# A four-layer hybrid block on one Trainium2 core: feed-forward weights unpacked in halves inside the last full phase, and a new order of the first two and last two phases

## The chip, the cores and the metric

The kernel runs on one core of one Trainium2 chip. Its time is the device time of one execution in microseconds (us). The engines named below are TensorE (PE, matmuls), VectorE (DVE), ScalarE (ACT), GpSimd (POOL) and the queue that issues the DMAs (SP). Each has its own stream of instructions and takes them in order; an instruction waits at the head of its stream until what it reads has been written and what it overwrites has been read.

## What is computed

The input x is 2 sequences of 512 tokens with 512 values each, in fp32. Four layers follow one another, each with a layer norm ahead and a residual sum behind:

```python
x = x + attn_a(layernorm(x))   # one 512x512 matmul with a block mask, and a bias
x = x + ffn(layernorm(x))      # silu(x@gate) * (x@up) @ down, weights stored as integers
x = x + attn_b(layernorm(x))   # the mixer: a state-space layer
x = x + ffn(layernorm(x))      # the same weights again
```

The feed-forward weights are unpacked as `(w - zero) * scale`, zero and scale per 128 rows; gate and up are 512x1792 each, down is 1792x512. In the mixer:

```python
gate, hBC, dt = split(x @ in_proj_w.T)     # 8192, 8192 + 2*8*128, 128 columns
hBC = silu(causal_conv4(hBC) + conv_b)
x, B, C = split(hBC)                       # 128 heads of 64; 8 groups of 128
dt = softplus(dt + dt_bias); A_dt = -exp(A_log) * dt
acs = cumsum(A_dt, within chunks of 128)
y = (tril(C B^T) * exp(acs_l - acs_s)) @ (x*dt)   # within a chunk
  + C @ state * exp(acs)                          # from the chunks before
  + D * x
y = y * rsqrt(mean(y^2) + eps) * norm_w * silu(gate)
return y @ out_proj_w.T
```

The factor rsqrt(mean(y^2) + eps) is one number per token, so the kernel applies it after the output projection, once the sum of squares over all 8192 values is known.

## The kernel before, in words

All four layers are one launch. `x_sb` holds the 1024 tokens in 8 tiles of 128 (t = 0 to 3 are sequence b = 0, 4 to 7 are b = 1), and `xn_t` the normalized input, transposed. `norm` (L102) makes statistics (L107, L109), the root on ACT (L111), the reciprocal (L114) and the scaled tile `tmp` (L121) on DVE; `turn` (L129) transposes it on PE into `ln_tr` (L134) and copies it to `xn_t` on ACT (L135). Most large projections go through `seven` (L169), the seven products of Strassen-Winograd in place of eight; its matmuls are all L177, its sums of products are L189 (ACT copy), L192, L197, L198, L206 and L211 (DVE).

The mixer (L532) works in phases. The 8192 inner channels are 64 tiles of 128; a phase takes two of them (j = 0, 1) for both sequences, so there are 32 phases. A phase's units are the four pairs (j, b). The loop over ph is software-pipelined: while the x columns of phase ph are projected and convolved (`x_front`; taps on DVE, L592, first tap on ACT, L589; silu L607), the tokens of phase ph - 1 are transposed (`x_tokens`, L685, L689, L693), its states formed (`states`, L706 to L717), its decay matrices (`half_scores`: `scores` with m on ACT, L747, L754, and DVE, L755, ce on ACT and POOL, L757, L761) and its scans done (`scan`: py, L774 and L783; y and gt, L793 and L794), and phase ph - 2 goes through the output projection (`out_project`, po, L808, added to `x_sb` by L818). The gates' stage of a phase (`g_front`: `seven` into `gt`, then silu) closes it. B and C belong to groups of eight channel tiles; a new group's `c_t`, `b_t` and `gm` are made every four phases (`group`, `group_scores`, L629 to L637). Squares of y are added up on POOL (`squares`, L800, L801).

The first phases stand ahead of the loop: `decays` (L557) makes the cumulative sums of a sequence and two exponentials of them, `step_sizes` the dt of the second sequence. The last phase (ph = 32, `front` false) breaks out of the loop and is written out below it: output projections of phase 30 (`outs`), scans of phase 31, `last_outs` (the output projections of phase 31), `factors` (L1064: ms, the sums of squares over 8192 on PE, L1067; root L99; reciprocal L100), `residual` (L1076: load of the stored input `x_d`, then L1079), and the norms of the next layer (`rest`, `ahead`). The second feed-forward layer then begins with pg and pu (L403) on slab 0 (256 columns), made from the weights that `first` holds. `dequant` (L222) loads integers, zeros and scales with three DMAs, subtracts on DVE (L230) and multiplies on POOL (L231).

The order on PE, ACT and DVE is the order in which the program names the instructions (`manual_schedule`, L1166). POOL's instructions and the DMAs on SP are ordered by the scheduler, from their priorities and from when their buffers come free. PSUM has three named sets of banks: `tr` (2), `proj` (3) and `yo` (3). `weights()` gives one of three 512 KB weight tiles, `room()` one of three 128x512 `tmp` tiles.

Of the kernel before, what the change touches and what calls it, by code (L numbers as in the profile page):

```python
# [8 lines left out]
F32 = mybir.dt.float32  # L9
# [28 lines left out]
def kernel(  # L38
# [210 lines left out]

    def now(q_compute):  # L250
        q, compute = q_compute
        compute()
        return q
# [229 lines left out]
    dt = keep.tile([P, NT, H], F32, tag="dt", name="dt")  # L483

    acs = keep.tile([P, NT, H], F32, tag="acs", name="acs")
# [46 lines left out]
    def mixer(waiting, step_args, loaded):  # L532

        with ExitStack() as st:
# [22 lines left out]
            def decays(b):  # L557

                cs = slice(b * NCH, (b + 1) * NCH)
                acs_t = room()  # L560
                pt = psum.tile([H, SEQ], F32, tag="tr", name="pacs")
                for c in range(NCH):
                    nc.tensor.matmul(
                        pt[:, c * P : (c + 1) * P],
                        lhsT=acs[:, b * NCH + c, :],
                        rhs=tri,
                        start=True,
                        stop=True,
                    )
                nc.scalar.copy(acs_t, pt)  # L570
                nc.sync.dma_start(acs_d[:, b * SEQ : (b + 1) * SEQ], acs_t)
                pa = psum.tile([P, NCH, H], F32, tag="yo", name="pa", bufs=3)
                pl = psum.tile([P, NCH, H], F32, tag="yo", name="pl", bufs=3)
                nc.tensor.matmul(pa, lhsT=tri, rhs=acs[:, cs, :], start=True, stop=True)
                nc.tensor.matmul(pl, lhsT=ones, rhs=acs[:, cs, :], start=True, stop=True)
                nc.scalar.copy(acs[:, cs, :], pa)
                nc.vector.tensor_tensor(
                    dec[:, b], pl[:, : NCH - 1], acs[:, b * NCH : (b + 1) * NCH - 1, :], ALU.subtract
                )
                nc.scalar.activation(e_last[:, b], pl[:, 1 : NCH - 1], AF.Exp)  # L580
                nc.scalar.activation(dec[:, b], dec[:, b], AF.Exp)
# [221 lines left out]
            def out_project(ph, ts, gts, wo):  # L803
                for t in ts:
                    b, c = divmod(t, NCH)
                    po = psum.tile([P, DIM], F32, tag="yo", name="po", bufs=3)
                    for j in range(PP):
                        nc.tensor.matmul(  # L808
                            po,
                            lhsT=gts[j, b][:, c * P : (c + 1) * P],  # L810
                            rhs=wo[:, j, :],
                            start=(j == 0),
                            stop=(j == PP - 1),
                        )
# [22 lines left out]
            decays(0)  # L837
# [3 lines left out]
            turn(waiting.pop(0))  # L841
            two_quarters(slice(SEQ - P, SEQ))
# [13 lines left out]
            decays(1)  # L856
# [3 lines left out]
            next(steps_bc)  # L860
            half_scores(0, 0, heads, ces)
# [4 lines left out]
            next(steps_bc)  # L866
            drain(3)
            next(steps_bc)
# [3 lines left out]
            half_scores(3, 0, heads, ces)  # L872
            run(steps_bc)
            gate, later = g_front(wg, gts)
            next(gate)
            drain(3)
# [3 lines left out]
            drain(3)  # L880
# [17 lines left out]
            first = []  # L898

            def scratch(shape):  # L900
                return [wrk.tile(shape, ty, tag="bc", name=nm, bufs=3) for nm, ty in (("wi", I32), ("zi", I32), ("sf", F32))]

            def scratch_up(shape):
                return [
                    pool.tile(shape, ty, tag=tag, name=nm)
                    for pool, tag, nm, ty in (
                        (sc, "wo", "wi", I32),
                        (keep, "dt", "zi", I32),
                        (keep, "acs", "sf", F32),
                    )  # L910
                ]

            for ph in range(1, n_ph + 1):
# [46 lines left out]
                wg = load_pair(c0, c0 + 1)  # L960
                if new_group:
                    wbc = load_group((c0 + PP) // CTG)
# [35 lines left out]
                finish(scans)  # L998
# [7 lines left out]
                for k in range(4):  # L1006
                    between(2 * k)
                    flush()
                    if last or k:
                        back_scores(4 + k)  # L1010
                    if last:
                        drain(1 if k < 3 else 0)
                    if made and k in (1, 2):
                        group_scores(made, groups[c0 // CTG], [k - 1])
                    between(2 * k + 1)
                    if last:
                        drain(1 if k < 3 else 0)
# [13 lines left out]
                if last:  # L1031
                    gate, later = g_front(wg, gts_new)
                finish(half_scan(units[2:], "proj" if new_group else "yo"))
                if last:
                    next(gate)
                half_scores(0, c0, heads_new)
                if last:
                    next(gate)
                drain(3)
# [47 lines left out]
            def last_outs(t):  # L1087
                out_project(n_ph - 1, [t], gts, wo_last)
# [3 lines left out]
            outs(0)  # L1092
            flush()
# [152 lines left out]
```

## Time and profile before

| what | value |
|---|---|
| time, three runs | 2327.41, 2327.43, 2330.75 us (median 2327.43) |
| the profiled execution's own time | 2327.67 us |
| its span in the profile | 2325.8 us (1.87 us lie around it) |
| mean granted PE clock | 0.996 |
| PE busy | 2296.2 us (99%) |
| DVE busy | 1607.5 us (69%) |
| ACT busy | 1155.2 us (50%) |
| POOL busy | 992.0 us (43%) |
| bytes moved by DMA | 201.41 MB |

The span runs from the first to the last recorded instruction. An engine's busy time is the part of the span in which it has an instruction in work. A line of the timeline gives start, duration, engine, line of the kernel, operation, output and inputs, the shape of both and how many instructions are taken together; brackets at its end hold the idle time just before it and what ended it. The mixer's first phase begins near 326 us, its last stage near 1998 us, and pg of the last feed-forward layer starts at 2050.14 us. The granted clock (PEclk) is TensorE's, 1.00 being full speed.

### The profile page before, as it was taken

What the parts mean: (1) busy time and instruction counts of PE and PEld (TensorE: products, weight loads), DVE (VectorE), ACT (ScalarE), POOL (GpSimd) and SP (SyncE); (2) the same over time, 40 slices, a digit from 0 to 9 for tenths busy, and PEclk for the clock granted to TensorE, in tenths of its full rate; (3) what the DMA queues carried; (4) which work ended last, traced back from release to release, by engine and by line L of the source; (5) the groups of instructions that cost most, each with busy time, mean ns of one, the idle gap of its engine ahead of it and who ended that gap; (6) DMA issues with size and microseconds to landing.
All of it is one profiled execution on the core that took longest, in us unless ns stands there. A gap on an engine that the chain in (4) does not pass through costs nothing.

```text
span 2325.8 us, 27474 instructions
## 1 busy us (share of the span) xinstructions
PE 2296.2 (99%) x9680; PEld 1214.3 (52%) x9680; DVE 1607.5 (69%) x2814; ACT 1155.2 (50%) x2460; POOL 992.0 (43%) x963
## 2 busy tenths in 40 slices
PE   9999998999999999999999999999999999899999
PEld 5444454555555555555555555555555555544444
DVE  5454148788788787877877887878778788755510
ACT  4111046656656665666565656556665666521100
POOL 2764013544544454444454444444453443346500
PEclk9999999999999999999999999999999999999999
DMA  5663012222222222222222222221222222346500
GB/s 185 191 200 100 23 55 77 73 73 73 73 82 64 73 82 73 64 73 82 68 69 81 73 65 78 78 73 64 82 72 65 75 71 73 91 141 216 176 14 23
DMA packets 145673, 201.41 MB, mean 87 GB/s; under 512 B 7040, under 2 KB 91904, under 8 KB 145536
## 3 DMA queue, kind: packets, MB, share of 16 engines
q1 hardware_dynamic: 145536, 199.66, 27.0%
q8 instruction: 77, 1.26, 0.2%
q14 instruction: 60, 0.49, 0.1%
HBM read 194.91 MB, written 4.72 MB: 86 GB/s over the span
## 4 chain that ended last, share of the span: by engine, by line
PE 95%; DVE 2%; DMA 1%; ACT 1%; issue 0%; SPq 0%; DVEq 0%; ACTq 0%
PE proj L177 39%; PE po L808 19%; PE yo L177 10%; PE ffn_o L453 8%; PE py L774 5%; PE pst L706 4%; PE py L783 3%; PE x_tr L685 2%; PE pg L403 1%; PE pu L403 1%; PE bs_o L305 1%; PE pgm L636 1%; DVE xc L592 1%; PE ln_tr L134 1%; DMA wi<-in_up_w_dram 0%
## 5 line engine op out<-in xcount | busy, mean ns | idle before, releaser
L761 POOL TENSOR_TENSOR ce<-ce,c_t 128x384 f32<-128x384 f32 x256 | 266.9, 1047 | 452.5 <-ACT ce L757 445.5
L808 PE MATMUL po<-wo,gt 128*128 128x512 f32 x992 | 436.8, 595 | 0.0
L177 PE MATMUL proj<-xn_t,w 128*128 128x512 f32 x912 | 424.9, 596 | 3.4 <-DVE gt L192 3.2
L747 ACT ACTIVATE m<-bc,acs 128x128 f32<-128x128 f32 x1024 | 324.6, 389 | 10.4 <-PE py L774 10.4
L808 PEld LDWEIGHTS po<-wo,gt 128*128 128x128 f32 x992 | 184.6, 190 | 219.6 <-issue 194.9
L177 PE MATMUL proj<-tq,ws 128*128 128x512 f32 x608 | 278.8, 592 | 1.3 <-DVE xc L592 1.3
L177 PEld LDWEIGHTS proj<-xn_t,w 128*128 128x128 f32 x912 | 165.6, 190 | 182.9 <-issue 171.3
L755 DVE TENSOR_TENSOR m<-m,gm 128x512 f32<-128x512 f32 x256 | 218.7, 875 | 0.0
L163 POOL TENSOR_TENSOR ws<-w 128x256 f32<-128x256 f32 x96 | 72.0, 750 | 335.3 <-DMA w<-in_win_t_dram 322.8
L592 DVE SCALAR_TENSOR_TENSOR xc<-proj,cw,xc 128x511 f32<-128x511 f32 (+2 forms) x288 | 213.2, 741 | 2.5
L453 PE MATMUL ffn_o<-down,h_t 128*128 128x512 f32 x448 | 193.4, 592 | 0.0
L693 POOL TENSOR_TENSOR x_dec<-x_dt,dec 128x384 f32<-128x384 f32 x128 | 130.8, 1031 | 133.6 <-DVE x_dt L689 128.1
L818 DVE TENSOR_TENSOR x_sb<-x_sb,po 128x512 f32<-128x512 f32 x248 | 167.8, 677 | 26.8 <-PE po L808 25.7
L801 POOL TENSOR_TENSOR sq_acc<-sq_acc,y 128x512 f32<-128x512 f32 x128 | 175.2, 1383 | 17.1 <-ACT y L800 16.9
L177 PEld LDWEIGHTS proj<-tq,ws 128*128 128x128 f32 x608 | 112.8, 190 | 131.6 <-issue 122.0
L774 PE MATMUL py<-m,x_dt 128*64 128x128 f32 x2048 | 181.4, 276 | 0.1
L754 ACT ACTIVATE m<-m 128x512 f32<-128x512 f32 x256 | 161.3, 630 | 7.4
L589 ACT ACTIVATE xc<-proj,cb,cw 128x512 f32<-128x512 f32 x96 | 71.2, 774 | 165.4 <-DVE proj L206 147.0
L783 PE MATMUL py<-ce,state 128*64 128x128 f32 x1536 | 149.9, 273 | 0.0
L177 PE MATMUL proj<-tq,w 128*128 128x512 f32 x304 | 143.0, 592 | 1.3 <-DVE gt L197 1.3
L177 PE MATMUL proj<-xn_t,ws 128*128 128x512 f32 x304 | 142.8, 592 | 0.0
L453 PEld LDWEIGHTS ffn_o<-down,h_t 128*128 128x128 f32 x448 | 84.7, 190 | 104.8 <-issue 104.8
(178 smaller groups left out, 3437.2 us busy)
## 6 DMA issues: line engine op xcount, KB each, us to landing
bc<-acs_d SPq DMA_DIRECT2D x128, 512.0 KB, 3.7
w<-in_win_t_dram SPq DMA_DIRECT2D x64, 512.0 KB, 3.8
wo<-in_wo_t_dram SPq DMA_DIRECT2D x31, 512.0 KB, 3.7
wi<-in_gate_w_dram SPq DMA_DIRECT2D x14, 512.0 KB, 4.1
zi<-in_gate_z_dram SPq DMA_DIRECT2D x14, 512.0 KB, 5.2
sf<-in_gate_s_dram SPq DMA_DIRECT2D x14, 512.0 KB, 5.2
wi<-in_up_w_dram SPq DMA_DIRECT2D x14, 512.0 KB, 4.9
zi<-in_up_z_dram SPq DMA_DIRECT2D x14, 512.0 KB, 6.0
```

What stands on the lines that cost most here:

```text
L177: nc.tensor.matmul(ps, lhsT=a[:, kc, :], rhs=b[:, kc, :], start=(start and kc == 0), stop=(stop and kc == KH - 1), skip_group_check=True,)
L453: nc.tensor.matmul(po, lhsT=h_t[:, fc, t * P : (t + 1) * P], rhs=down[:, fc, :], start=(fc == 0), stop=(fc == NFC - 1),)
L592: nc.vector.scalar_tensor_tensor(dst[:, s:], ps[:, : SEQ - s], cw[:, t, 3 - s : 4 - s], dst[:, s:], ALU.mult, ALU.add)
L747: nc.scalar.activation(m[:, c, :], bc[:, hh, c * P : (c + 1) * P], AF.Relu, bias=acs[:, t, h : h + 1], scale=-1.0,)
L754: nc.scalar.activation(m, m, AF.Exp, scale=-1.0)
L755: mults.append(lambda: nc.vector.tensor_mul(m, m, shared[b][2]))
L761: nc.gpsimd.tensor_mul(ce, ce, c_t[:, P:].rearrange("p (c l) -> p c l", l=P))
L774: nc.tensor.matmul(py[hh * HD : (hh + 1) * HD, c * P : (c + 1) * P], lhsT=x_dt[:, c, hh, :], rhs=m[:, c, :], start=True, stop=(c == 0),)
L783: nc.tensor.matmul(py[hh * HD : (hh + 1) * HD, c * P : (c + 1) * P], lhsT=state[:, c - 1, hh, :], rhs=ce[:, c - 1, :], start=False, stop=True,
L801: nc.gpsimd.tensor_add(sq_acc[:, b, :], sq_acc[:, b, :], y)
L808: nc.tensor.matmul(po, lhsT=gts[j, b][:, c * P : (c + 1) * P], rhs=wo[:, j, :], start=(j == 0), stop=(j == PP - 1),)
L818: nc.vector.tensor_add(acc[:, t, :], acc[:, t, :], po)
```

## The change

Five things are changed; the loop's middle phases keep their order on all engines.

1. **First two phases.** `decays` returns its two exponentials as a function, and they are called later. The score half 3 of phase 0 moves behind the first step of the gates, one `drain(3)` (convolution taps) moves behind a step of the group projection, one is dropped, so that its taps come with the next. In phase 1, `finish(scans)` (the y and gt of the first two units) moves into the loop over k, behind the gates' steps, and silu of the new x columns moves ahead of `half_scores(0, ...)`.
2. **Unpacking.** Slab 0 of gate and up is unpacked in halves of two 128-row blocks (`dequant_half`), each half with three DMAs of 256 KB. The loads of the gate's halves are named at the start of phase 31, into the old group's `c_t`, `b_t` and `gm` tiles; the first up half goes into the three `tmp` tiles, the second into the old group's tiles again. Sub and mult are called in the gates' stage of phase 31, the second up half's after the first `outs` of the last stage. Before, both whole slabs were loaded and unpacked among the last output projections.
3. **Residual.** The eight loads of `x_d` are named in the last stage, behind the scores' loads, into the old `xc` and `gt` tiles, and no longer into a `y` room just ahead of their use.
4. **Order of the end.** On PE: projections 0, 1, ms, 2, both scans, 3, turn 0, 4, turn 1, 5, turn 2, 6, turn 3, 7, ms. Before: 0, 1, 2, ms, 3, both scans, turn 0, turn 1, 4, 5, turn 2, 6, 7, turn 3, ms.
5. **Banks.** In the last stage the scans' py and the projections of t = 4, 6, 7 use `proj` banks in place of `yo`.

```diff
+    def dequant_half(q, h, s, w, z, sc, scratch):
+
+        cols = slice(s * SLAB, (s + 1) * SLAB)
+        rows, ks = slice(h * KH * P, (h + 1) * KH * P), slice(h * KH, (h + 1) * KH)
+        shape = [P, KH, SLAB]
+        return dequant(
+            q[:, ks].rearrange("p kc j c -> p kc (j c)"),
+            w[rows, cols].rearrange("(kc p) i -> p kc i", p=P),
+            z[ks, cols],
+            sc[ks, cols],
+            scratch(shape),
+            shape,
+        )
...
-                nc.scalar.activation(e_last[:, b], pl[:, 1 : NCH - 1], AF.Exp)
-                nc.scalar.activation(dec[:, b], dec[:, b], AF.Exp)
+
+                def exponentials():
+                    nc.scalar.activation(e_last[:, b], pl[:, 1 : NCH - 1], AF.Exp)
+                    nc.scalar.activation(dec[:, b], dec[:, b], AF.Exp)
+
+                return exponentials
...
-            def out_project(ph, ts, gts, wo):
+            def out_project(ph, ts, gts, wo, tag="yo"):
...
-            decays(0)
+            exps = decays(0)
             turn(waiting.pop(0))
             next(steps)
             two_quarters(slice(0, SEQ - P))
             turn(waiting.pop(0))
+            exps()
...
-            decays(1)
+            exps = decays(1)
             groups[0] = []
             ces = []
             steps_bc, made = group(0, wbc, "yo")
             next(steps_bc)
+            exps()
             half_scores(0, 0, heads, ces)
             drain(3)
             next(steps_bc)
             drain(3)
             half_scores(1, 0, heads, ces)
             next(steps_bc)
+            next(steps_bc)
             drain(3)
-            next(steps_bc)
             half_scores(2, 0, heads, ces)
             next(steps_bc)
             next(steps_bc)
-            half_scores(3, 0, heads, ces)
             run(steps_bc)
             gate, later = g_front(wg, gts)
             next(gate)
+            half_scores(3, 0, heads, ces)
             drain(3)
             next(gate)
             drain(3)
             next(gate)
-            drain(3)
             for u in units:
                 silu(xcs[u], xcs[u])
             next(gate)
...
+            old_group = places((grp, "c_t0", 2), (grp, "c_t1", 2), (grp, "b_t0", 1))
+            old_scores = places((grp, "b_t1", 1), (grp, "gm0", 2), (grp, "gm1", 2))
+            old_tmp = places(*[(keep, "tmp", 3)] * 3)
...
                 wg = load_pair(c0, c0 + 1)
+                final = ph == n_ph - 1
+                if final:
+
+                    gate_q = weights()
+                    gates = [
+                        dequant_half(gate_q, h, 0, gate_w, gate_z, gate_s, r)
+                        for h, r in enumerate((old_group, old_scores))
+                    ]
...
                     gate, later = g_front(wg, gts_new)
-                finish(scans)
+                else:
+                    finish(scans)
...
                     between(2 * k + 1)
+                    finish(scans)
...
                     gate, later = g_front(wg, gts_new)
+                if final:
+                    up_q = weights()
+                    ups = [dequant_half(up_q, 0, 0, up_w, up_z, up_s, old_tmp)]
                 finish(half_scan(units[2:], "proj" if new_group else "yo"))
                 if last:
                     next(gate)
+                else:
+                    for u in units:
+                        silu(xcs_new[u], xcs_new[u])
                 half_scores(0, c0, heads_new)
                 if last:
                     next(gate)
+                if final:
+                    for f in gates:
+                        f()
+                    ups.append(dequant_half(up_q, 1, 0, up_w, up_z, up_s, old_group))
                 drain(3)
                 half_scores(1, c0, heads_new)
                 if last:
                     next(gate)
-                for u in units:
-                    silu(xcs_new[u], xcs_new[u])
-                if last:
+                    for u in units:
+                        silu(xcs_new[u], xcs_new[u])
                     next(gate)
                 drain(3)
                 flush()
+                if final:
+                    next(gate)
+                    ups[0]()
                 run(gate)
...
+            xrs = []
+            for t in range(NT):
+                j, b = divmod(t % 4, 2)
+                xr = act.tile([P, SEQ], F32, tag=f"{'xc' if t < NCH else 'gt'}{j}{b}", name="xr")
+                xrs.append(xr)
+
+            def load_residual(t):
+                nc.sync.dma_start(xrs[t], x_d[t * P : (t + 1) * P, :])
+
             def residual(t):
-                xr = y_room()
-                nc.sync.dma_start(xr, x_d[t * P : (t + 1) * P, :])
                 nc.vector.scalar_tensor_tensor(
-                    x_sb[:, t, :], acc[:, t, :], rn[:, t : t + 1], xr, ALU.mult, ALU.add
+                    x_sb[:, t, :], acc[:, t, :], rn[:, t : t + 1], xrs[t], ALU.mult, ALU.add
                 )
...
-                out_project(n_ph - 1, [t], gts, wo_last)
+                out_project(n_ph - 1, [t], gts, wo_last, "proj" if t in (4, 6, 7) else "yo")
...
             outs(0)
+            ups[1]()
             flush()
...
-            finish(half_scan(units[:2]))
             back_scores(4)
+            for t in range(NCH):
+                load_residual(t)
+            finish(half_scan(units[:2], "proj"))
             outs(6)
             back_scores(5)
             outs(7)
             flush()
+            for t in range(NCH, NT):
+                load_residual(t)
             all_squares()
             both_states(1)
             back_scores(6)
             last_outs(0)
+            flush()
             last_outs(1)
+            back_scores(7)
+            factors(0)
+            last_outs(2)
             flush()
-            back_scores(7)
-            last_outs(2)
-            factors(0)
-            last_outs(3)
-            flush()
-            gate = dequant_gate(0, scratch)
-            up = dequant_up(0, scratch_up)
-            scans = half_scan(units[2:])
             half = rest(0)
...
+            scans = half_scan(units[2:], "proj")
             normed = ahead(0)
             finish(scans)
+            last_outs(3)
             turn(normed)
-            turn(ahead(1))
+            normed = ahead(1)
             all_squares()
             last_outs(4)
-            first.append(now(gate))
+            turn(normed)
             normed = ahead(2)
             last_outs(5)
             turn(normed)
-            first.append(now(up))
+            normed = half()
             last_outs(6)
-            normed = half()
+            turn(normed)
             last_outs(7)
-            turn(normed)
             factors(1)
+            first = [gate_q, up_q]
```

More of the change, by code (lines that the diff above doesn't have):

```diff
@@ L480, in load_group @@
         return load_pair(2 * NCT + g, 2 * NCT + G + g)
-    dt = keep.tile([P, NT, H], F32, tag="dt", name="dt")
-    acs = keep.tile([P, NT, H], F32, tag="acs", name="acs")
+    dt = keep.tile([P, NT, H], F32, name="dt")
+    acs = keep.tile([P, NT, H], F32, name="acs")
     def step_weights():
@@ L801, in squares @@
                 nc.gpsimd.tensor_add(sq_acc[:, b, :], sq_acc[:, b, :], y)
-            def out_project(ph, ts, gts, wo):
+            def out_project(ph, ts, gts, wo, tag="yo"):
                 for t in ts:
                     b, c = divmod(t, NCH)
-                    po = psum.tile([P, DIM], F32, tag="yo", name="po", bufs=3)
+                    po = psum.tile([P, DIM], F32, tag=tag, name="po", bufs=3)
                     for j in range(PP):
@@ L897, in mixer, with places, scratch @@
             gts_old = None
[L898 to L911, printed above, removed]
+            def places(*at):
+                def scratch(shape):
+                    return [
+                        pool.tile(shape, ty, tag=tag, name=nm, bufs=bufs)
+                        for (pool, tag, bufs), nm, ty in zip(at, ("wi", "zi", "sf"), (I32, I32, F32))
+                    ]
+                return scratch
+            old_group = places((grp, "c_t0", 2), (grp, "c_t1", 2), (grp, "b_t0", 1))
+            old_scores = places((grp, "b_t1", 1), (grp, "gm0", 2), (grp, "gm1", 2))
+            old_tmp = places(*[(keep, "tmp", 3)] * 3)
             for ph in range(1, n_ph + 1):
@@ L960, in mixer @@
                 wg = load_pair(c0, c0 + 1)
+                final = ph == n_ph - 1
[4 more added lines that the diff above has]
+                        for h, r in enumerate((old_group, old_scores))
+                    ]
                 if new_group:
```

## The prediction, made before the result was known

> **What bounds the kernel now.** I read the page's shares and its chain first, then TensorE's (PE's) waits by window, then PE's timeline where waits stand, then VectorE (DVE) beside it.
>
> ```profile
> PE 2296.2 (99%) x9680; PEld 1214.3 (52%) x9680; DVE 1607.5 (69%) x2814; ACT 1155.2 (50%) x2460; POOL 992.0 (43%) x963
> ...
> PE   9999998999999999999999999999999999899999
> ...
> PE 95%; DVE 2%; DMA 1%; ACT 1%; issue 0%; SPq 0%; DVEq 0%; ACTq 0%
> ```
>
> PE is the bound, and only two slices of its row fall below nine tenths. It idles 2325.8 - 2296.2 = 29.6 us in all. From 430 to 2013 us its list of waits is empty, so nothing can be won there without removing matmuls, and the change removes none. Two places hold 21.6 us of the idle time. First, the waits from 320 to 430 us (line waited for: total us, times, longest):
>
> ```profile
> PE proj L177 <- DVE gt L192: 3.2, 2, 2.8
> PE x_tr L685 <- ACT xc L607: 2.1, 1, 2.1
> PE proj L177 <- DVE gt L197: 1.3, 1, 1.3
> PE yo L177 <- DVE tmp L197: 1.3, 1, 1.3
> PE proj L177 <- DVE xc L592: 1.3, 2, 1.0
> ```
>
> With 0.66, 0.25, 0.35 and 0.21 us of smaller ones these are 10.7 us. PE's timeline gives what one costs:
>
> ```profile
> 402.70 1.95 PE L177 MATMUL proj<-tq,ws 128*128 128x512 f32 x4 [0.27 <-DVE xc L592]
> 407.42 3.70 PE L177 MATMUL proj<-xn_t,w 128*128 128x512 f32 x8 [2.76 <-DVE gt L192]
> 410.95 1.88 PE L177 MATMUL proj<-tq,w 128*128 128x512 f32 x4
> ```
>
> Four matmuls are spaced 1.72 us start to start when fed. Ahead of the wait they last 1.95 (0.23 over), and the eight after it take 3.53 until the next start instead of 3.44: a wait costs 0.32 over its idle. DVE shows why L192 is late: two y/gt pairs and an m stand ahead of it.
>
> Second, 2013 us to the end (DVE's tmp L121 is the layer norm's scaled tile; ln_tr its transpose):
>
> ```profile
> 2027.09 0.74 PE L134 MATMUL ln_tr<-ident,tmp 128*128 128x128 f32 x4 [2.09 <-DVE tmp L121]
> 2032.21 1.09 PE L134 MATMUL ln_tr<-ident,tmp 128*128 128x128 f32 x4 [4.39 <-DVE tmp L121]
> 2033.09 5.90 PE L808 MATMUL po<-w,gt 128*128 128x512 f32 x8
> 2041.87 1.09 PE L134 MATMUL ln_tr<-ident,tmp 128*128 128x128 f32 x4 [2.88 <-DVE tmp L121]
> 2042.74 6.19 PE L808 MATMUL po<-w,gt 128*128 128x512 f32 x8
> ...
> 2050.14 3.67 PE L403 MATMUL pg<-xn_t,w 128*128 128x512 f32 x8
> ```
>
> Idle 9.36 us, and eight matmuls last 5.90 and 6.19 where they last 3.60 elsewhere. The windows (PEclk is the column before the DMA share) say why:
>
> ```profile
> 2020.00:2030.00 10.00, 5.74 (x64) 3.94 (x63) 8.11 (x16) 1.44 (x4) 0.00 (x0) 0.87 0.21 59
> 2030.00:2040.00 10.00, 6.78 (x12) 3.12 (x12) 5.14 (x9) 1.93 (x4) 3.88 (x3) 0.61 0.24 79
> 2040.00:2050.00 10.00, 8.13 (x24) 4.54 (x24) 5.41 (x9) 1.47 (x3) 3.78 (x2) 0.66 0.09 26
> ```
>
> The granted clock halves here. That costs 2.3 + 2.6 on the projections and about 0.6 on transposes: 5.5 us which the list of waits does not show.
>
> [...] 2.76 idle at 404.7 left the clock at 1.00. [...] The trace shows loads of 1.28 with the next activation right behind (418.41 to 419.71), so I use 1.28. [...] L755 takes 0.68 alone and up to 1.3 beside POOL; L121 0.55, and 1.45 at 2040.27 beside L231.
>
> **The change, the end of the mixer.** From the first last-phase projection (2013.86) to pg (2050.14) PE takes 36.3 us. Its work there is 8 projections x 1.72 = 13.8, two ms 1.7, two scans 3.1, four transposes 0.44 each = 1.8; sum 20.3. Lost: 9.4 idle + 5.5 clock + 1.1 refills.
>
> New order: projections 0, 1, ms, 2, scans, then 3, turn 0, 4, turn 1, 5, turn 2, 6, turn 3, 7, ms. PE passes the scans at 2023.1 (1.7 earlier, projection 3 being moved behind) and ends projection 3 at 2024.8. DVE, on its own rows: rn after the earlier ms at 2018.7; add 2 to 2020.6; m 0.6; residual 0 (0.75) and its statistics (0.9) to 2022.8; the same for 1 to 2024.4; reciprocal and tmp 0 to 2025.05: PE waits 0.3 where it waited 2.09. Then y, gt twice (4 x 0.75) to 2027.9; projection 4 needs both gt: waits of 1.0 and 0.55, ended 2028.8. Then add 3, residual 2, statistics, reciprocal, tmp 1 (0.69 + 0.75 + 0.9 + 0.13 + 0.55 = 3.0) to 2030.9: 2.1 waited for 4.39. A further such 3.0 to 2033.9 for tmp 2: projection 5 covers all but 0.8 of it (was 2.88). tmp 3 is covered by projection 6. Sum of waits 4.75; with 20.3 of work and 0.3 of refill 25.3: pg starts at 2039.15, **11.0 earlier**, provided that the clock stays up: the longest wait is 2.1, below the 2.88 that halved it.
>
> The early residual loads take away DVE's wait for DMA y<-x_d (1.43 at 2054.21) and so PE's 0.82 at 2058.80: with refill **1.1**. The 0.73 for xn_t stays. Projections 4, 6, 7 and the scans on proj banks take no time by themselves: they let a projection start while the add of an older one is still queued.
>
> **Unpacking moved to the gates' stage of phase 31.** DVE: 2 x 1.22 at the end become 4 x 0.65 (half of L230). Two stand behind L192 (1983.98) in 2.67 idle ahead of L197, one in 0.82 idle ahead of L206, one in 1.03 ahead of an add at 1996.81: nothing. Without that cover, 2.6. Each now waits at DVE's head for three DMAs: behind the gate halves stands L197, behind the first up half L206, for which PE waits next. The gate halves are issued when the old group's tiles come free, about 1816 to 1831, the first up half near 1960; both are long landed by 1984. The second is rival four. POOL: 2 x 2.35 to 2.78 become 4 x 1.2 to 1.5, in 10.29 and 5.51 idle there; ce waits 1.3 longer, but it is needed a half stage later: nothing. SP: 6 DMAs of 512 KB become 12 of 256 KB. The gate halves' waits on freed group buffers are met at 1824.7 to 1831.1, before the bc load behind them would issue (1840.0); a later bc stands behind POOL's gate half at 1987.4, issued before at 1987.30. Nothing is passed late. Eight residual loads are issued behind the scores' loads, tiles free by then: nothing, or 4 us of DMA if PE outran them, still 20 us ahead of use. wo_last reaches a freed slot at about 1992, lands in 3.7, needed at 2013.9: nothing.
>
> **The first two phases.** PE's order is kept; DVE's and ScalarE's (ACT's) changes. Exponentials later: 0.66 and 0.25 go, but the step-size chain behind them gives back part: 0.75. L197/L198 ahead of the taps: 1.32 goes. Gates: score half 3 behind the gate's first copy and the last drain(3) dropped: 0.40 and 1.34 go. L192 ahead of the y/gt pairs: 2.76 goes (y/gt are next needed by the squares, later). ACT's silu(xc) ahead of the scores, in its 5.97 idle before 416.04: 2.12 goes; two more table loads (2 x 1.28) fit there, but the copy to tmp then comes late, a new wait of about 1.2 (DVE's L192 of the next tile waits for that copy, an x_dt behind it, and PE for L192). Taps at 1.05, 0.27, 0.35 stay. Sum 0.75 + 1.32 + 0.40 + 1.34 + 2.76 + 2.12 - 1.2 = 7.5, and about four refills x 0.32: **8.7**. Bounds: 9.5 if the new wait is covered, 5 if ACT's loads land on its path twice.
>
> **Sum.** 11.0 + 1.1 + 8.7 = 20.8. My tables use undisturbed DVE times; two contended operations (0.65 each) on the two chains take 1.3: **19.5**. The profiled run took 2327.67 (span 2325.8 and 1.87 around it), so 2308.2; the median of the runs is 0.24 lower: **2308.0**.
>
> **Rivals.**
> 1. The clock halves again. After 2024.8 PE is busy 2.2 us of the next 6.1[...]. Price: one stretch as before, 2.4, with DVE 1.6 later; front 6.3 for 8.7. Gain 12.1 - 4.0 + 6.3 = 14.4: 2313.0.
> 2. The front isn't won: DVE is 97% busy from 396 to 404 us and ACT 99% from 416 to 424, so a wait on one tile becomes a wait on the next. Front 3, end 6.4: 2318.
> 3. It doesn't do what it says: norms stay late because DVE's chain, not order, sets each 3.0. Only the residual loads and little else remain: 2325.
> 4. Slower. The second up half is loaded only when POOL has multiplied a gate half (1987.3); landing takes 6.0 (median of zi in the up loads), so 1993.3, with 3.5 to spare to its place in DVE's queue, ahead of the add at 1996.81. If it lands later, adds, x_dt and the whole last stage queue behind, PE one for one. It decides when the loss passes 19.5 + 4.7, a landing at about 2021; at 2033 the time is 2340. The DMA share of 0.21 to 0.41 around there speaks against it.
>
> **How the numbers follow.** Forecast 0.63 (by itself 2304 to 2311.5), rival one 0.24, two 0.07, three 0.03, four 0.03. The range 2303 to 2317 holds the forecast and rival one. A measurement tells 0.2% (4.7 us) from no change: faster means below 2322.8 (0.94), same is rival three (0.03), slower rival four (0.03).
>
> **What would show it.** After: ln_tr waits near 0.3, 2.1, 0.8; a pg start 10 to 12 before that of now, counted from the first last-phase projection; projections of 3.6, not 5.9; waits for L197, L192 (2.8) and x_tr gone by 430 us, tap waits kept; the stretch between as long as before. Wrong if DVE waits for DMA in the gates' stage of phase 31, if the clock column stays at 0.6, or if the front's idle only changes its name.

## The result, and the profile after

| | before | after |
|---|---|---|
| median of the runs | 2327.42 us (2325.08 to 2330.75, 4 runs) | 2308.88 us (2307.23 to 2309.23, 4 runs) |
| profiled run, its span | 2327.67, 2325.8 us | 2307.23, 2305.2 us |
| PE busy | 2296.2 us | 2288.9 us |

The ratio is 0.9922 (95% interval 0.991 to 0.9934): 18.5 us faster. The forecast was 2308.0 us, 19.5 faster.

The page of the changed kernel, its shares and its chain:

```profile
PE 2288.9 (99%) x9680; PEld 1210.6 (53%) x9680; DVE 1608.5 (70%) x2816; ACT 1158.3 (50%) x2462; POOL 994.9 (43%) x965
...
PE   9999999999999999999999999999999999999999
...
PE 97%; DVE 2%; DMA 0%; ACT 0%; issue 0%; SPq 0%; DVEq 0%
```

The two weak slices of PE's row are gone. PE has as many instructions as before but is busy 7.3 us less: that is no work removed, but matmuls that no longer run at half clock (in before the granted clock was 0.50 from 2042 to 2046 us, where eight projections took 6.19 us for 3.60) or last longer ahead of a wait, and 0.6 us of warm-up matmuls (see below). PE's waits from 320 to 430 us, in the changed kernel:

```profile
PE proj L177 <- DVE xc L611: 1.3, 2, 1.1
PE proj L177 <- DVE gt L197: 0.8, 1, 0.8
PE proj L177 <- DVE gt L206: 0.5, 1, 0.5
PE x_tr L704 <- DVE x_dt L708: 0.5, 1, 0.5
PE yo L177 <- ACT acs L591: 0.4, 1, 0.4
PE x_tr L704 <- DVE gm L656: 0.3, 1, 0.3
```

The waits for L192 (2.8), for silu (2.1) and for tmp L197 are gone; the taps' 1.3 stays, as forecast. Two names are new (L206, x_dt), and L197 is back at another place with 0.8. Together 3.9 us where 10.7 stood. The list of waits between 430 us and the last stage is still empty. From 1990 us on:

```profile
PE ln_tr L134 <- DVE tmp L121: 3.3, 3, 1.8
PE po L827 <- DVE gt L813: 1.0, 2, 0.7
PE pg L417 <- ACT xn_t L135: 0.7, 1, 0.7
```

And PE's timeline there:

```profile
2004.61 3.60 PE L827 MATMUL po<-w,gt 128*128 128x512 f32 x8
...
2016.11 0.63 PE L134 MATMUL ln_tr<-ident,tmp 128*128 128x128 f32 x4 [0.17 <-DVE tmp L121]
2017.46 1.12 PE L827 MATMUL po<-w,gt 128*128 128x512 f32 x2 [0.72 <-DVE gt L813]
2018.91 1.12 PE L827 MATMUL po<-w,gt 128*128 128x512 f32 x2 [0.32 <-DVE gt L813]
2021.84 0.63 PE L134 MATMUL ln_tr<-ident,tmp 128*128 128x128 f32 x4 [1.80 <-DVE tmp L121]
2022.30 1.88 PE L827 MATMUL po<-w,gt 128*128 128x512 f32 x4
2025.52 0.63 PE L134 MATMUL ln_tr<-ident,tmp 128*128 128x128 f32 x4 [1.34 <-DVE tmp L121]
...
2030.67 3.68 PE L417 MATMUL pg<-xn_t,w 128*128 128x512 f32 x8
```

The waits for tmp are 0.17, 1.80 and 1.34 (forecast 0.3, 2.1, 0.8), for gt 0.72 and 0.32 (1.0 and 0.55). Four matmuls take 1.88 here, and the granted clock is 1.00 from 2000 to 2040 us.

Single executions differ, so the kernels below are compared by three stretches of PE's timeline: from the mixer's first L177 to the first last-phase projection (L), from there to the first pg (G), and to the first L177 of slab 1 (S).

| profiled run | first L177 | to L | L to G | G to S |
|---|---|---|---|---|
| before | 326.23 | 1687.63 | 36.28 | 31.60 |
| after | 324.84 | 1679.77 | 26.06 | 30.29 |
| difference | -1.39 | -7.86 | -10.22 | -1.31 |

The sum of the last three is 19.4 us. The 1.39 ahead of them is not the change's: it lies in the first 20 us, which the change doesn't touch (the kernel's own warm-up matmuls took 8.27 in the run of before and 7.67 in this one; a wait of 0.87 for DVE in the first layer is absent here). So the two spans differ by 20.6, and the change explains 19.4 of it. The profiled run of after is also the fastest of its four; between medians the gain is 18.5.

### The profile page after: what moved, and what is told of

The parts are those of the page before. It is cut to its first block, busy times and chain, and to the rows that moved or that the text cites. A ratio compares the mean times of both kernels' runs of the same rounds, so it can differ in the third digit from the quotient of the medians.

```text
span 2305.2 us, 27492 instructions
## 1 busy us (share of the span) xinstructions
PE 2288.9 (99%) x9680; PEld 1210.6 (53%) x9680; DVE 1608.5 (70%) x2816; ACT 1158.3 (50%) x2462; POOL 994.9 (43%) x965
## 4 chain that ended last, share of the span: by engine, by line
PE 97%; DVE 2%; DMA 0%; ACT 0%; issue 0%; SPq 0%; DVEq 0%
PE proj L177 39%; PE po L827 19%; PE yo L177 10%; PE ffn_o L467 8%; PE py L793 5%; PE pst L725 4%; PE py L802 3%; PE x_tr L704 2%; PE pg L417 1%; PE pu L417 1%; PE bs_o L319 1%; PE pgm L655 1%; PE ln_tr L134 1%; DVE xc L611 0%; PE pd L521 0%
## 5 line engine op out<-in xcount | busy, mean ns | idle before, releaser
L177 PE MATMUL proj<-xn_t,w 128*128 128x512 f32 x912 | 424.8, 596 | 0.5 <-DVE gt L206 0.5
L177 PE MATMUL proj<-tq,ws 128*128 128x512 f32 x608 | 278.8, 592 | 1.3 <-DVE xc L611 1.3
L177 PEld LDWEIGHTS proj<-xn_t,w 128*128 128x128 f32 x912 | 165.7, 190 | 179.5 <-issue 171.8
L774 DVE TENSOR_TENSOR m<-m,gm 128x512 f32<-128x512 f32 x256 | 220.9, 883 | 0.4 <-ACT m L773 0.4
L177 PEld LDWEIGHTS proj<-tq,ws 128*128 128x128 f32 x608 | 112.8, 190 | 131.6 <-issue 122.2
L177 PE MATMUL proj<-tq,w 128*128 128x512 f32 x304 | 143.0, 592 | 0.8 <-DVE gt L197 0.8
L177 PE MATMUL proj<-xn_t,ws 128*128 128x512 f32 x304 | 142.8, 592 | 0.0
```

Of the source, the lines that this page charges most:

```text
L177: nc.tensor.matmul(ps, lhsT=a[:, kc, :], rhs=b[:, kc, :], start=(start and kc == 0), stop=(stop and kc == KH - 1), skip_group_check=True,)
L774: mults.append(lambda: nc.vector.tensor_mul(m, m, shared[b][2]))
```

## Experiments

**1. The front alone.** The kernel before with the hunks of `decays`, of phase 0 and of phase 1 (`finish(scans)`, silu) and nothing else.

> The kernel before with the new order of its first two phases alone. Theory (waits removed in the front are won for good, since PE is always busy behind them): the first projection of the last phase comes about 8 us earlier, counted from the mixer's first L177; from there to pg still 36.3 us; time about 2319.5. Rival (the gain is given back by waits on other tiles or further on): less than 3 us, 2324.5 or more.

Measured: 2318.36 us (4 runs), ratio 0.9954 (0.994 to 0.9969). To L 1679.75 us, as in the changed kernel; L to G 34.61. The front's 7.9 us are won for good and need nothing of the end. (The half clock at the end fell otherwise in this run: the two groups of eight projections took 4.77 and 5.29 us where before had 5.90 and 6.19, and the three waits for tmp were 0.9 longer in sum, hence 34.61 and not 36.28.)

**2. The unpacking alone.** The kernel before with `dequant_half`, `places`, `gates` and `ups`, and without:

```diff
-            gate = dequant_gate(0, scratch)
-            up = dequant_up(0, scratch_up)
...
-            first.append(now(gate))
...
-            first.append(now(up))
...
+            first = [gate_q, up_q]
```

> The kernel before with the unpacking in halves in the gates' stage of phase 31 alone; order, banks and residual loads of the end as before. Theory (order and unpacking share the end): tmp of the third norm comes some 2.1 us earlier without L230 ahead of it and without POOL beside it, PE's wait of 2.88 falls to about 0.4, and the second stretch of half clock does not come: gain about 5, time about 2322.5; the first stretch stays. Rival (unpacking was nearly all of the end): gain of 8 or more, 2319 or less. Rival (it does nothing without the order): within 1 of before.

Measured: L to G 31.13 us in the profile, 5.15 less. The third norm's tmp is waited for 0.95, and the second group of eight projections is back at 3.60, as expected:

```profile
2034.94 1.09 PE L134 MATMUL ln_tr<-ident,tmp 128*128 128x128 f32 x4 [4.17 <-DVE tmp L121]
2035.82 5.78 PE L822 MATMUL po<-w,gt 128*128 128x512 f32 x8
2042.55 0.63 PE L134 MATMUL ln_tr<-ident,tmp 128*128 128x128 f32 x4 [0.95 <-DVE tmp L121]
2043.01 3.60 PE L822 MATMUL po<-w,gt 128*128 128x512 f32 x8
```

But the median of 20 runs is 2324.35 us, only 2.9 below the 2327.28 of before in the same batch (0.9984, 0.9977 to 0.9991). In the profiled run (2325.52 us) the clock fell in two places that this kernel doesn't change. One is in the front:

```profile
408.88 5.25 PE L177 MATMUL proj<-xn_t,w 128*128 128x512 f32 x8 [2.76 <-DVE gt L192]
```

In the profile of before, the same eight matmuls behind the same 2.76 us took 3.70. The other is in the first layer, where the first two matmuls at 22.83 us (L319) took 1.82 us; in before they took 1.02. They start 0.48 us earlier than in before, while the mixer's first L177 stands at 327.44, 1.21 later: 1.7 us are lost between. Together these two cost 3.2 us of the 5.15; the span is only 2.3 us shorter than that of before. The nine runs whose mean granted clock reads 0.998 or 0.999 took 2321.3 to 2322.9 us, the other eleven (0.995 or 0.996) 2324.1 to 2328.0. Only one run has a trace, so where the others lost their time is not shown.

**3. The order alone.** New order of the end, banks and early residual; the old front, and the old unpacking, called behind projection 4 and behind turn 2 (shown against the changed kernel; its loads are left out here):

```diff
             last_outs(4)
+            first.append(now(gate))
             turn(normed)
             normed = ahead(2)
             last_outs(5)
             turn(normed)
+            first.append(now(up))
```

> The kernel before with the new order of the end, the banks and the early residual loads, but the old unpacking (both slabs loaded late, sub and mult among the last projections) and the old front. Theory: the end's gain of about 11 less 1.2 to 1.5 us of L230 ahead of the third norm, 0.9 of POOL beside it and perhaps 2 us of half clock: gain 7 to 9, time about 2319.5. Rival (the unpacking sets the end): gain under 4, over 2323.

Measured: 2321.87 us (7 runs), ratio 0.9973 (0.9962 to 0.9985), 5.4 faster: below the 7 to 9 of the theory, above the rival's 4. L to G is 31.46 us, 4.8 less, and G to S 30.29, 1.3 less. What the unpacking costs here is above all one wait, for the third norm's tmp: 4.46 where the changed kernel has 1.34 (the fourth norm's is waited for 0.43 more).

```profile
2038.12 0.63 PE L134 MATMUL ln_tr<-ident,tmp 128*128 128x128 f32 x4 [4.46 <-DVE tmp L121]
2038.59 3.54 PE L808 MATMUL po<-w,gt 128*128 128x512 f32 x4
```

The clock also fell behind that wait: four matmuls take 3.54 for 1.88. From L to G, order and unpacking give 4.8 and 5.15 alone and 10.2 together, so in the profiles they add up. Neither was the end's one cause. Between medians the three parts alone give 8.9 (front), 2.9 and 5.4, in sum 17.3, where the whole change gives 18.5.

**4. What the half clock costs.** The kernel before with matmuls added in three of PE's waits (`stir`; their results are not used, and the trace shows each as two records), to keep the clock up. First 12, 30 and 18, then, since one takes 0.223 us and these ran past the waits, 8, 17 and 12:

```diff
             finish(scans)
+            stir(8)
             turn(normed)
+            stir(17)
             turn(ahead(1))
...
             last_outs(5)
+            stir(12)
             turn(normed)
```

> The kernel before with 60 idle-time matmuls of 128x128 added in three of PE's waits at the end (12, 30 and 18), nothing else changed; their results are not used. Theory (the half clock costs 5.5 us that the list of waits does not show): the clock stays at 1.00, the two groups of eight projections take 3.60 instead of 5.90 and 6.19, time about 2322.5 with the same norm chain. Rival (the clock is not what those groups wait for, or filling only delays the transposes): no gain, 2327 or more.

> The kernel before with fewer added matmuls in PE's waits at the end (8, 17 and 12, at 0.223 us each as measured with 12, 30 and 18), so that they end before the tiles that PE waits for. Theory (the half clock costs 5.5 us at the end): the clock stays up, both groups of eight projections take 3.60, and from the first last-phase projection to pg 31 us instead of 36.3; time about 2322. Rival (what the clock gives back DVE's chain takes, since tmp of the third norm does not come earlier): 33.5 us or more and 2325 or more.

Measured, the first: clock 1.000 in the profiled run, both groups at 3.60, but no gain, 2326.74 us (0.9999, 0.9992 to 1.0006): the 6.7 us of added work in a wait of 4.39 took it back. The second: 2324.95 us (21 runs), 0.9991 (0.9984 to 0.9997), and L to G 32.69, that is 3.6 us less: the theory said 31, which is 5.3 less, the rival at most 2.8. PE's timeline of the second:

```profile
2032.12 3.60 PE L808 MATMUL po<-w,gt 128*128 128x512 f32 x8
2035.55 2.84 PE L219 MATMUL stir<-ones 128*128 128x128 f32 x24
2040.17 0.63 PE L134 MATMUL ln_tr<-ident,tmp 128*128 128x128 f32 x4 [1.77 <-DVE tmp L121]
2040.63 3.60 PE L808 MATMUL po<-w,gt 128*128 128x512 f32 x8
```

The first group is 2.3 us faster, yet tmp comes only 1.2 earlier. DVE's timeline shows what took the rest: the residual behind the earlier add now runs beside POOL's squares and lasts 1.75 instead of 0.75.

```profile
2034.64 1.22 DVE L230 TENSOR_TENSOR w<-wi,zi 128x1024 f32<-128x1024 int32 x1
2035.78 1.75 DVE L1079 SCALAR_TENSOR_TENSOR x_sb<-x_sb,rn,y 128x512 f32<-128x512 f32 x1
```

So in this profile the 5.5 us by which matmuls were stretched were worth 3.6 us on the path to pg in the old order. The median fell by only 1.9 us, close to the rival's 2325: the profiled run took 2323.52, while 8 of the 21 took 2326.9 us or more at a clock of 0.997 to 0.999. Where those lost time is not shown.

**5. The residual loaded just in time.** The changed kernel with the old `residual`, which loads just ahead of its use into a `y` tile (a y room).

> The changed kernel with the residual loaded just in time into a y room again, as before. Theory of the prediction (the early loads are worth 1.1 us, the wait of the fourth residual of the second half): 1.1 to 1.4 us slower than the changed kernel, about 2310. Rival (in the new order a y room comes free only when POOL has added the second scans' squares, so the fourth residual of the first half waits for its load too): tmp of that norm some 4 us later, 2313 to 2315.

Measured: 2309.92 us (5 runs), 1.0 above the changed kernel; L to G 26.07, unchanged; G to S 31.63, 1.3 more. DVE waits once more for the fourth residual of the second half, and nowhere long in the first:

```profile
2036.14 0.75 DVE L1122 SCALAR_TENSOR_TENSOR x_sb<-x_sb,rn,y 128x512 f32<-128x512 f32 x1 [1.35 <-DMA y<-x_d]
```

The prediction's term is right; the rival (a y room held up by the squares) is not.

**6. One set of banks.** The changed kernel with `"proj"` taken out of the last projections and scans.

> The changed kernel with all last projections and scans on yo banks, as before. Theory (banks take no time by themselves: each add is done before its bank is asked for): within 1 us of the changed kernel, about 2309, and no wait of po or py for an add. Rival (a projection or py waits for the add of an older one, DVE being full there): 2 to 4 us slower, with a wait po or py <- DVE x_sb in PE's list.

Measured: 2308.18 us (4 runs), L to G 26.21 (0.15 more), no wait for an add. The banks alone are worth nothing here. But in this profile (mean granted clock 0.999) the clock fell behind the 1.80 us wait, and projection 5 took 3.16 for 1.88:

```profile
2021.93 1.07 PE L134 MATMUL ln_tr<-ident,tmp 128*128 128x128 f32 x4 [1.80 <-DVE tmp L121]
2022.79 3.16 PE L827 MATMUL po<-w,gt 128*128 128x512 f32 x4
2025.79 0.60 PE L134 MATMUL ln_tr<-ident,tmp 128*128 128x128 f32 x4
```

That cost next to nothing, since the stretched work filled the wait for the next tmp. The same happened in the profile of experiment 7 (3.02 for that projection, L to G 26.08). So the event of rival one came in two of the five profiles with this order of the end and this unpacking, without the price that rival one put on it.

**7. Phase 0 and phase 1 apart.** The changed kernel with the hunks of phase 1 undone.

> The changed kernel with phase 1 ordered as before: finish(scans) ahead of the gates again and silu of the new columns behind the scores; phase 0 and the end as changed. Prediction's table: phase 0 gives 4.7 and phase 1 4.0, so 4.0 slower, about 2313. Reading of the trace after: phase 1 gave 3.5, so 2312.4. Rival (phase 1 only shifts waits onto the copy to tmp): under 1.5 slower.

Measured: 2314.13 us (5 runs), 5.3 above the changed kernel. To L 1684.46 us, 4.7 more than after; 1.7 of it is half clock behind the wait that came back:

```profile
403.26 5.39 PE L177 MATMUL proj<-xn_t,w 128*128 128x512 f32 x8 [2.77 <-DVE gt L192]
```

Eight such matmuls took 3.70 in before. Without that stretch phase 1 is worth 3.0 us and phase 0 4.9 (4.0 and 4.7 by the prediction's terms).

**8. Where a kernel's runs differ.** Two experiments share a version with another order of the end: the second scans' y and gt ahead of the second norm, projections ahead of turns, and the adds of projections 4 to 7 behind the last scaled tile. `adds` holds the adds of the projections until they are named.

```diff
-            scans = half_scan(units[2:], "proj")
-            normed = ahead(0)
-            finish(scans)
-            last_outs(3)
-            turn(normed)
-            normed = ahead(1)
-            all_squares()
-            last_outs(4)
-            turn(normed)
-            normed = ahead(2)
-            last_outs(5)
-            turn(normed)
-            normed = half()
-            last_outs(6)
-            turn(normed)
-            last_outs(7)
+            adds = []
+            finish(half_scan(units[2:], "proj"))
+            all_squares()
+            for t in (3, 4, 5):
+                last_outs(t, adds)
+            normed = ahead(0)
+            turn(normed)
+            adds.pop(0)()
+            normed = ahead(1)
+            last_outs(6, adds)
+            turn(normed)
+            normed = ahead(2)
+            last_outs(7, adds)
+            turn(normed)
+            turn(half())
+            for f in adds:
+                f()
```

> The changed kernel with another order of the end: the second scans' y and gt ahead of the second norm, projections 4 to 7 each ahead of a turn as early as gt allows, and the adds of projections 4 to 7 behind the last scaled tile. Theory (after the change PE waits 4.3 us there because DVE is full, and nothing that PE can do is held back but by order; adds of 4 to 7 don't belong on the norms' chain): pg 22.5 to 23.5 us after the first last-phase projection instead of 26.1, time about 2306. Rival (DVE's chain of norms sets pg whatever the order): pg at 25 or later, within 1 us of the changed kernel.

Measured: 2305.39 us, ratio to before 0.9909 (0.9894 to 0.9925). L to G 22.76 us, 3.3 less than in the changed kernel; PE's waits there fall from 4.35 to 1.0:

```profile
2013.90 5.57 PE L827 MATMUL po<-w,gt 128*128 128x512 f32 x12
2019.97 0.63 PE L134 MATMUL ln_tr<-ident,tmp 128*128 128x128 f32 x4 [0.51 <-DVE tmp L121]
2020.43 1.88 PE L827 MATMUL po<-w,gt 128*128 128x512 f32 x4
2022.80 0.63 PE L134 MATMUL ln_tr<-ident,tmp 128*128 128x128 f32 x4 [0.48 <-DVE tmp L121]
```

So the changed kernel's last waits were due to the order too. The interval overlaps the changed kernel's; the runs do not (2303.93 to 2307.07 against 2307.23 to 2309.23), and the one-bank kernel, measured in the same batch and equal to the changed one by its trace, took 2308.18.

Its four runs took 2303.97, 2306.82, 2303.93 and 2307.07 us, with granted clocks of 1.000, 0.999, 1.000 and 0.999. A mean of 0.999 over 2300 us is, as an estimate from these two numbers, a few us at half speed. In the two profiled runs of experiments 2 and 3 such a stretch stands in the first layer, behind two waits near 20 us. In experiment 3:

```profile
19.36 0.66 PE L134 MATMUL ln_tr<-ident,tmp 128*128 128x128 f32 x4 [0.46 <-ACT tmp L119]
21.41 1.11 PE L134 MATMUL ln_tr<-ident,tmp 128*128 128x128 f32 x4 [1.39 <-ACT tmp L119]
```

The second transpose takes 1.11 us, where it takes 0.66 in before. Nine matmuls were added to the waits there:

```diff
+                if kc == 2:
+                    stir(3)
                 product(0, pos[0], kc)
...
+                    if t < 2:
+                        stir((1, 5)[t])
                     turn(ahead)
```

> The kernel of the run with the other order of the end, and nine added matmuls of 128x128 (results unused) in three of PE's waits between 12 and 23 us, in the first layer. It tests where the spread of a kernel's runs comes from. Theory [...]: every run reads a granted clock of 1.000, all lie within 1 us of each other, near 2304, the lower of the two groups of the kernel without the added matmuls (2303.9 and 2306.9). Rival (the spread comes from elsewhere, a load's landing for one): two groups remain, or the clock reads 0.999 in some runs as before.

Measured: 2304.78, 2304.52, 2304.30, 2304.57 us, all at 1.000; median 2304.54, ratio 0.99 (0.9884 to 0.9917). The two groups become one, as the theory said. It is the fastest version here. But four runs are few (if the upper group came in half of all runs by chance, four runs would still miss it once in 16 times), the four were taken on another chip than those without the added matmuls, and neither run of the upper group has a trace. The stretch in experiment 2 cost 1.7 us, while the groups lie 3 us apart. So that the waits near 20 us part the groups is likely, and what makes up the rest is open.

**9. A later load.** The changed kernel with the second up half loaded into the tmp tiles, after the first up half was multiplied.

```diff
-                    ups.append(dequant_half(up_q, 1, 0, up_w, up_z, up_s, old_group))
...
                     ups[0]()
+                    ups.append(dequant_half(up_q, 1, 0, up_w, up_z, up_s, old_tmp))
```

> The changed kernel with the second up half loaded only when the first has been multiplied (into the tmp tiles), some 6 us later than now. It tests the price of rival four. Rival four as the prediction put it (every us of lateness costs PE one): DVE waits about 2 to 3 us for this load ahead of the second add, PE loses as much, 2311 to 2312. Other view (DVE has 0.3 to 1 us of idle time ahead of each of the next adds, and three banks lie between PE and an add): the wait is in DVE's list, but PE loses less than 1 us, about 2309.

Measured: 2308.54 us (5 runs), as the changed kernel (0.9918, 0.9905 to 0.9932). The loads are issued at 1983.98 to 1985.34, in the changed kernel at 1976.05 to 1978.59 (in this run everything there stands 1.6 us later), yet DVE waits only 0.33 for them:

```profile
1988.45 1.16 DVE L230 TENSOR_TENSOR w<-wi,zi 128x512 f32<-128x512 int32 x1 [0.33 <-DMA zi<-in_up_z_dram]
```

Rival four had DVE waiting 2 to 3 us here. But the zeros landed 3.9 us after their issue, not 6.0, and the margin in the changed kernel was some 6.5 us, not 3.5. The price of rival four beyond that margin wasn't tried.

## Why the prediction was right, step by step

**Sum.** 19.4 us in the two profiles and 18.5 between medians, against 19.5. The mechanisms held: each wait that was to go went or shrank, and order, unpacking, residual and front each gained time by themselves. Three terms were off and partly cancelled, so that the sum came so close is in part luck.

**End of the mixer.** Forecast 11.0, measured 10.2. The waits came smaller than written (4.35 for 4.75). The term that was too small is "0.3 of refill": five waits at 0.16 to 0.27 each, and 0.17 between projection 2 and the scans, are 1.3. The prediction had itself measured 0.32 over a wait's idle in the front, and used it for five waits as though there were one. The half clock did not come in this profile, as assumed, but that was luck: experiments 6 and 7 show it behind the same 1.80 us wait. So "below the 2.88 that halved it" was no safe reason. The end was won all the same, since there it cost next to nothing. In before, the two slow transposes cost 0.4 us each and the first 0.1, so the clock's share was nearer 5.8 than 5.5 and the refills' so much less; the total of 36.3 stays.

**Residual.** Forecast 1.1, measured 1.3 (and 1.3 in experiment 5, by itself). Right.

**The front.** Forecast 8.7, measured 7.9. The waits that were to go are gone (8.85 us with the first two counted whole), and about 1.0 is left for refills (1.2 forecast). The new waits are the term that was too small: 1.2 forecast, 2.0 measured, and PE does not wait for the copy to tmp (DVE does, 1.44 at 417.64). In phase 0, taps now stand ahead of L206: 0.53, and acs is waited for 0.40 where it was 0.21. In phase 1, PE waits 0.51 for an x_dt at 415.75, behind two m operations on DVE that took 2.62 us where two take 1.28 undisturbed. And moving the y/gt pairs behind L192 puts them ahead of L197; beside POOL the last gt takes 1.54 instead of 0.75, and L197 comes 0.78 late:

```profile
398.13 0.68 DVE L192 TENSOR_TENSOR gt<-gt,proj 128x512 f32<-128x512 f32 x1
398.73 0.73 DVE L812 SCALAR_TENSOR_TENSOR y<-xc,dsk,py 128x512 f32<-128x512 f32 x1
399.50 0.96 DVE L813 SCALAR_TENSOR_TENSOR gt<-y,nw,gt 128x512 f32<-128x512 f32 x1
400.38 0.73 DVE L812 SCALAR_TENSOR_TENSOR y<-xc,dsk,py 128x512 f32<-128x512 f32 x1
401.15 1.54 DVE L813 SCALAR_TENSOR_TENSOR gt<-y,nw,gt 128x512 f32<-128x512 f32 x1
402.62 0.68 DVE L197 TENSOR_TENSOR gt<-gt,proj 128x512 f32<-128x512 f32 x1
```

Rival two had named this ("a wait on one tile becomes a wait on the next"), but with a price that was too high: phase 1 still won 3.0. The prediction asked what is late next only behind ACT's silu; of the y/gt pairs on DVE it said that they are next needed by the squares, and did not ask what they stand ahead of. That is the step it missed.

**Contention.** The 1.3 us set aside for DVE beside POOL is about what came: 0.8 on that gt, and in the end 0.85 on the residual of the third tmp, part of which is in its wait of 1.34 (0.8 forecast). The measured 10.2 and 7.9 already contain it, so the sum of 20.8 less 1.3 met the result because the contention, the missing refills and the new waits together cost 1.4. Of the prediction's examples of contention, L755 reaches 1.49 in the trace of before, not 1.3.

**Unpacking.** Forecast at nothing, and PE waits for nothing in that stage. The cover was thinner than written, though. DVE's two subtractions for the gate (L230) took 2.09 us instead of 1.3, and the two m operations (L774) 2.33 instead of 1.28, beside POOL: of the 2.67 us idle ahead of L197 0.67 is left, of the 0.82 ahead of L206 nothing:

```profile
1975.34 2.09 DVE L230 TENSOR_TENSOR w<-wi,zi 128x512 f32<-128x512 int32 x2
1978.09 0.69 DVE L197 TENSOR_TENSOR gt<-gt,proj 128x512 f32<-128x512 f32 x1 [0.67 <-PE proj L177]
...
1979.42 2.33 DVE L774 TENSOR_TENSOR m<-m,gm 128x512 f32<-128x512 f32 x2
1981.68 0.68 DVE L230 TENSOR_TENSOR w<-wi,zi 128x512 f32<-128x512 int32 x1
1982.28 0.68 DVE L206 TENSOR_TENSOR gt<-gt,proj 128x512 f32<-128x512 f32 x1
```

**Rivals.** One (half clock again) did not come in the profile, and where it came (experiments 6 and 7) its price of 4.0 at the end did not. Two of the changed kernel's four runs read 0.999, and at most 2 us lie between its runs. Which stretch of it is hit in those runs is open, since only one run has a trace. Two named the right mechanism in the front with too high a price. Three and four did not happen: the norms moved with the order (experiments 3 and 8), and the second up half had time to spare (experiment 9). (By rival four's own rule a landing at 2033 gives 2344 us, not 2340.) The price of the half clock, 5.5 us in the prediction, is the sum of the stretched matmuls; on the path to pg it was 3.6 in one profile, and 1.9 between medians (experiment 4).

## What to carry to other kernels

Where the bound engine idles only in a few places, list each wait, name what stands ahead of the releasing instruction in its engine's order, and ask after every move what is now late behind it on the same engine. Price a wait as its idle time plus what its refill costs, once for every wait (0.16 to 0.32 us here). Work that hides in the idle time of a shared stage uses up more of it than its undisturbed time says: here two pairs of DVE operations took 1.6 and 1.8 times as long beside POOL. So count on about half of the cover that the idle times promise.

## What the runs showed of the hardware

Behind a wait of 2.76 us eight matmuls took 3.70 us in before, 5.25 in experiment 2; behind 2.77 they took 5.39 in experiment 7. Behind a wait of 1.80 us four matmuls took 1.88 in four profiles (the changed kernel, experiments 3, 5 and 9) and 3.16 and 3.02 in two (6 and 7). So the length of a wait did not decide alone whether the clock fell, and the prediction had asked only how long the longest wait is. What else decided is not shown.

Such a stretch cost 1.5 to 1.7 us where PE had work to do (experiments 2 and 7) and next to nothing where the next tile was late anyway (6 and 7: L to G 26.21 and 26.08 us against 26.06). That runs of one kernel differ by such stretches fits the clocks and times of experiment 2 (0.998 or 0.999 in runs of up to 2322.9 us, 0.995 or 0.996 from 2324.1 us on), but is not shown, since one run of each kernel has a trace.
